# A graph layer and an expert layer on one core: the placing product moved to the end of TensorE's step, its addition behind VectorE's weighing

## The chip, the cores and the metric

The kernel runs on one NeuronCore of a Trainium2 chip. The metric is the device time of one execution in microseconds (us). Before the change it is 1864.92 us, the median of 7 runs (1861.53 to 1869.43).

## What is computed

The input is a matrix `x` of 6250 nodes with 256 values each and a list of 100,000 edges (`src`, `dst`), sorted by `dst`. Two layers are computed. The first is a graph attention layer with 8 heads: every node gathers the rows of the nodes that point to it, weighed by a softmax over its incoming edges, and a feed-forward net follows. The second sends every node through the two best of eight expert networks. In the reference, cut to what matters here:

```python
xn = layer_norm(x, ln1_g, ln1_b)
h = (xn @ W).reshape(N, HEADS, HEAD_DIM)
e = jax.nn.leaky_relu(a_src[src] + a_dst[dst], NEG_SLOPE)
ee = jnp.exp(e - emax[dst])
alpha = ee / denom[dst]
msg = h[src] * alpha[:, :, None]
agg = jax.ops.segment_sum(msg, dst, num_segments=N)      # the change is in how this sum is made
out = agg.reshape(N, HEADS * HEAD_DIM) + xn @ W_res + bias
out = layer_norm(out, ln2_g, ln2_b)
out = out + gelu_tanh(out @ ffn_w1 + ffn_b1) @ ffn_w2 + ffn_b2
# then, for every node: router, top 2 of 8 experts, weighted sum of their outputs
```

## The kernel before

**Preparation.** Up to about 150 us the kernel normalizes `x`, multiplies it by `W`, and writes a table of rows (`tab_s`: 256 values and 16 factors of the attention) to device memory. It also cuts the 782 tiles of 128 edges into 196 edge steps of four tiles. Since the edges are sorted by their target, the targets of some consecutive tiles lie close together. One to eight consecutive steps form a group, of which there are 110. The four tiles of a step write to four windows of 32 target rows each, and a whole group writes to at most 128 consecutive target rows, which straddle at most two of the 128-row blocks of the accumulators `acc_lo` and `acc_hi`. Groups are worked off from the last to the first: 66 groups with one step each, 31 with two, 9 with four and 4 with eight.

**The hand-written loop.** The loop at L1573 runs over a step number `s`. In each pass it issues one stage of several edge steps (a software pipeline, the list `STAGES` at L922), and after them, by `run_tasks` (L953), as many tasks of the node units and expert blocks as a budget per engine allows (`room`, from `ROOM` at L68; edge work is taken off it by `EDGES` and `BEHIND`). The stages of an entry `(f, d)` work on edge step `s - d`. Every engine executes its instructions in the order in which they are issued here; each engine has its own queue, and waits for another engine only where data or a buffer demand it. The stages are:

- `fetch` (L818, GpSimd): four indirect transfers that gather the source rows of an edge step into `gs` (four buffers).
- `spread` (L829, VectorE): the one-hot matrix `oh` of an edge step's targets within their windows; with the first step of a group also `qd`.
- `turn_spread` (L844, TensorE, then ScalarE): turns `oh` round in `pt` (one buffer, which the transpositions of the units, L982, share) and copies it.
- `give` (L851, TensorE): the product `pz`, which brings the targets' factors to the edges.
- `weigh` (L858, VectorE): three instructions, which multiply the gathered rows by their weights (`msg`).
- `add_tiles` (L872, TensorE): four products into `pl` (one buffer), summed over the steps of a group; behind the last step of a group ScalarE copies `pl` to `part` (two buffers).
- `place` (L896, VectorE, last step of a group only): the one-hot matrix `oh2` (two buffers) that says where the group's 128 sums belong within a block.
- `add_nodes` (L903, TensorE, last step of a group only): the placing product `p2` from `oh2` and `part`, at L906. `p2` has one buffer.
- `sum_up` (L910, VectorE, last step of a group only): reads the block's number into a register (L913), and adds `p2` to two neighbouring blocks by two instructions at L917.

**The order around the change.** Within a pass TensorE gets: `add_tiles`, `turn_spread`, `give`, `add_nodes`, then the tasks. VectorE gets: `sum_up` (of the product that TensorE got one pass earlier), `weigh`, `place`, `spread`, then the tasks.

**The tasks.** A first unit (L1187) multiplies two tiles of nodes by `W_res` into `py` (L1167, TensorE), and VectorE empties `py` with a bias added (`rg`, L1173). A node unit (L1207) divides the sums (L1054), normalizes them, and runs the feed-forward net: transpositions into `pt` (L982), a copy to `turned_in` by ScalarE (L989), products `ph` (L997), the gelu by ScalarE (`ht`, L1000), products `py` (L1007), which VectorE takes up (L1087). Then it normalizes again, routes (L1131 to L1145), and for every two units counts, ranks and lists tokens (up to `enlist`, L1323), a long run of small VectorE instructions. An expert block runs the same net with weights loaded for it, and VectorE empties `py` into `yb` (L1504). `py` has one buffer for all of them: a product into it can be issued in the same pass in which VectorE empties it, and waits for that.

Of the kernel before, what the change touches and what calls it, by code (L numbers as in the profile page):

```python
# [222 lines left out]
def gnn_moe_kernel(  # L223
# [66 lines left out]
    NG = len(order)  # L290
# [508 lines left out]
    def fetch_nodes(c):  # L799

        gq = bw.tile([P, W32 * 2 * H], F32, name="gq", bufs=1)
        nc.gpsimd.indirect_dma_start(
            out=gq, out_offset=None, in_=tab_q,
            in_offset=bass.IndirectOffsetOnAxis(ap=qrow[:, c:c + 1], axis=0))
        nc.sync.dma_start(tab_g[c * P:(c + 1) * P, :], gq)
        n = min(GC, NQ - c * GC)
        gd = bw.tile([P, GC, 2 * H], F32, name="gd")
        nc.sync.dma_start(gd[:, :n], tab_g[c * P:c * P + n * G, :].rearrange(
            "(g j) (r c) -> (j r) g c", j=G, r=W32))
        gds[c] = gd  # L810
# [91 lines left out]
    @behind_group  # L902
    def add_nodes(q):  # L903
        part, oh2 = live.pop((q, "part")), live.pop((q, "oh2"))
        p2 = bps.tile([P, DA], F32, name="p2")
        nc.tensor.matmul(p2, oh2, part, start=True, stop=True)  # L906
        live[q, "p2"] = p2

    @behind_group
    def sum_up(q):  # L910
# [4 lines left out]
        for b in range(2):  # L915
# [3 lines left out]

    STAGES = ((sum_up, 6), (weigh, 3), (add_tiles, 4), (place, 4), (turn_spread, 1), (give, 2),  # L922
              (spread, 0), (add_nodes, 5), (fetch, 0))
    LASTST = 6


# [26 lines left out]
    def run_tasks(s, room):  # L953

        more = True
        while more:
            more = False
            for t in list(pending):
                if (t.take in held or room[t.eng] <= 0.0
                        or any(d.step is None or d.step + gap > s for d, gap in t.deps)):  # L960
                    continue
                pending.remove(t)
                t.step = s
                room[t.eng] -= t.cost
                if t.take:
                    held.add(t.take)
                if t.free:
                    held.remove(t.free)
                t.fn()
                more = True  # L970
# [216 lines left out]
    def first_unit(u):  # L1187
        t0, n, _ = units[u]
        env = {}
        first_loads.append(task(lambda: load_first(t0, n, env), "SP", 0.0,  # L1190
                                [(d, 0) for d in back(firsts, 2)]))
        pr = task(lambda: first_product(n, env), "PE", 0.95 * n, [(first_loads[-1], 2)], take="py")
        ab = task(lambda: add_biases(n, env), "DVE", 0.7 * n,
                  [pr, *[(d, 0) for d in back(firsts, 1)]], free="py")
        firsts.append(task(lambda: store_first(t0, n, env), "SP", 0.0, [ab]))
# [3 lines left out]
    def node_loads(u):  # L1199
        t0, n, _ = units[u]  # L1200
        env = {"n": n}
        loads.append(task(lambda: load_nodes(t0, n, env), "SP", 0.0,
                          [(firsts[u], 0), *[(d, 0) for d in back(turned, 2) + back(added, 2)
                                             + back(normed, 3) + back(stores, 3)]]))
        return env
# [314 lines left out]
    def block_loads(i):  # L1520
        b = turn_of[i]
        env = {"n": 1 if NF <= b < NS else 2}
        env["units"], needs = next((u, d) for n, u, d in sure if n > b)
        free = [(d, 0) for d in blocks[i - 3:i - 2] + notes[i - 3:i - 2]] if i >= 3 else []

        env["pool"] = 1 if len(moew) > 1 and 1 not in pools[-2:] else 0
        user = [j for j in range(i) if pools[j] == env["pool"]][-2 + env["pool"]:][:1]
        if env["pool"] == 0 and pools.count(0) < 2:
            user = []
        pools.append(env["pool"])  # L1530
        env["lw"] = task(lambda: load_weights(b, env), "SP", 0.0,
                         [needs[-1], *[blocks[j] for j in user]])
        env["lx"] = task(lambda: load_block(b, env), "SP", 0.0, [*needs, *free])
        env["lp"] = task(lambda: load_params(b, env), "DVE", 0.4, [needs[-1], *free])
        ahead.append((b, env))
# [32 lines left out]
    s, u, since, was_nodes, loaded = 0, 0, [], False, {}  # L1568

    with tc.manual_schedule():  # L1570
        nc.sync.dma_start(xs[E * CAP:, :].rearrange("(p r) d -> p r d", r=2),
                          blank[:, None, :].to_broadcast([P, 2, DX]))
        while s < NG + LASTST or pending or u < len(units) or len(blocks) < NS:  # L1573
            for g in range(s, min(s + EARLY, NG)):
                if order[g][0] // GC not in gds:
                    fetch_nodes(order[g][0] // GC)
            for f, d in STAGES:
                if 0 <= s - d < NG:
                    f(s - d)
            if s == NG + LASTST:  # L1580
                edges.close()
                moew.append(gnn.enter_context(tc.tile_pool(name="moew3", bufs=1)))
            if len(firsts) < len(units) and len(firsts) <= s + 1:
                first_unit(len(firsts))
            if len(firsts) == len(units) and firsts[-1].step is not None and fp:
                first_.close()
                fp = None
            if last_hi and last_hi[0].step is not None and not moew and not fp:
                hi_pool.close()
                moew.append(ctx.enter_context(tc.tile_pool(name="moew", bufs=2, side="right")))  # L1590
            nb = len(blocks) + len(ahead)
            if moew and len(ahead) < 1 + len(moew) and nb < NS and any(n > turn_of[nb]
                                                                       for n, _, _ in sure):
                block_loads(nb)

            while sum(t.cost for t in pending if t.eng == "PE") < QUEUE:
                if (u < len(units) and units[u][2] <= s - LASTST
                        and not (ahead and was_nodes)):
                    was_nodes = True

                    if u == len(units) - 1:
                        urgent.append(0)
                    if u not in loaded:
                        loaded[u] = node_loads(u)
                    node_unit(u, loaded[u])
                    since.append(u)
                    u += 1
                    if u < min(len(units), len(firsts)):
                        loaded[u] = node_loads(u)
                    if u % 2 == 0 or u == len(units):  # L1610
                        chunk_tasks(since, u == len(units), u == len(units) - 1)
                        since = []
                    urgent.clear()
                elif ahead:
                    was_nodes = False
                    block_unit(*ahead.pop(0))
                else:
                    break
            room = dict(ROOM if s < NG + LASTST else ROOM_AFTER)
            if s < NG + LASTST:  # L1620
                g = s - 5
                ends = 0 <= g < NG and order[g][1] == groups[order[g][0]][1] - 1
                for e in EDGES:
                    room[e] -= EDGES[e] + ends * BEHIND[e]
            run_tasks(s, room)
            s += 1
            if there is None and final_list and final_list[0].step is not None and len(blocks) > NS - 2:
                there = nc.values_load(total[0:1, 0:1], min_val=0, max_val=NX)
        if NS < NX:
            with tc.If(there > NS):  # L1630
                while pending or len(blocks) < NX:
                    nb = len(blocks) + len(ahead)
                    if len(ahead) < 2 and nb < NX:
                        block_loads(nb)
                    if ahead:
                        block_unit(*ahead.pop(0))
                    run_tasks(s, dict(ROOM_AFTER))
                    s += 1
# [31 lines left out]
```

## Time and profile before

| | |
|---|---|
| median of 7 runs | 1864.92 us |
| profiled execution, its time | 1865.22 us |
| its span, first to last instruction | 1863.3 us |
| TensorE products busy | 1597.3 us, 86% |
| VectorE busy | 1080.1 us, 58% |
| GpSimd busy | 1113.7 us, 60% |
| ScalarE busy | 702.1 us, 38% |
| granted TensorE clock, mean | 0.942 |
| placing product L906: busy, idle before it | 82.4 us, 64.0 us, of them 63.9 for the addition L917 |
| addition L917 (220 instructions): busy, idle before them | 108.3 us, 127.3 us |

In profile lines the engines are PE (TensorE), PEld (its weight loads), DVE (VectorE), ACT (ScalarE) and POOL (GpSimd). A line of the timeline gives start and duration in us, engine, code line, operation, output and inputs, shape and count; in brackets stands the idle time of the engine just before it and what ended it. A line of the waits gives who waited for whom, total us, how often, and the longest. A line of a stretch gives its bounds and length, the busy time and the number of instructions of each engine, the granted clock of TensorE, the share of the DMA engines and GB/s. A float32 product is recorded as two matmul instructions. "issue" is time in which an engine waited for nothing that the profile shows.

### The profile page before, as it was taken

Reading aid. Unit: us, or ns where it says so; the run is one execution under the profiler, and the core shown is the slowest. Engines: PE = TensorE matmul, PEld = TensorE weight load, DVE = VectorE, ACT = ScalarE, POOL = GpSimd, SP = SyncE. Lnnn points to the kernel's source line nnn. Section 1 sums busy time; section 2 is a strip of 40 time slices with the busy share of each in tenths; the row PEclk is TensorE's granted clock in tenths of the full one; section 3 lists DMA queues with packets and bytes.
Section 4 is the critical chain, followed back from the end, with each engine's and each line's share of the span. In section 5 each row is a group of like instructions: output and inputs, shape, how many; then the busy total and the mean of one; then the engine's idle time right before and its main releaser. Section 6 shows DMA issues by size and latency. Waiting matters only on the chain. (4 is left out here: it accounts for less than half of the span.)

```text
span 1863.3 us, 28221 instructions
## 1 busy us (share of the span) xinstructions
PE 1597.3 (86%) x8479; PEld 1228.8 (66%) x8479; DVE 1080.1 (58%) x3959; ACT 702.1 (38%) x1621; POOL 1113.7 (60%) x1162
## 2 busy tenths in 40 slices
PE   4844787878787899999999999999999999899996
PEld 3523565656555677777777777777677777778885
DVE  8835888888888876575757564635544544131000
ACT  3830233233232343443444343443434433343332
POOL 2017765766656677767677777777777773321112
PEclk8977898889897999999999999999999999999998
DMA  3968755565445575756667666766668768648661
GB/s 117 294 206 219 232 159 152 165 173 175 146 141 169 155 225 156 232 155 189 173 175 213 200 184 192 225 196 206 207 187 248 224 154 227 200 104 274 188 190 39
DMA packets 246622, 347.86 MB, mean 187 GB/s; under 512 B 46033, under 2 KB 202865, under 8 KB 246460
## 3 DMA queue, kind: packets, MB, share of 16 engines
q1 hardware_dynamic: 184268, 203.16, 34.0%
q0 software_dynamic: 58880, 139.32, 29.2%
q10 hardware_dynamic: 3312, 3.48, 0.6%
q8 instruction: 70, 1.15, 0.3%
q14 instruction: 92, 0.75, 0.1%
HBM read 282.50 MB, written 67.26 MB: 188 GB/s over the span
## 5 line engine op out<-in xcount | busy, mean ns | idle before, releaser
L824 POOL DMA_INDIRECT gs<-tab_s,srce x784 | 803.5, 1025 | 349.8 <-issue 203.0
L997 PE MATMUL ph<-turned_in,w1b 128*128 128x256 f32 (+1 forms) x1696 | 388.8, 381 | 23.0 <-ACT ht L1000 17.6
L1007 PE MATMUL py<-w2b,ht 128*128 128x256 f32 x1648 | 370.8, 383 | 0.0
L997 PEld LDWEIGHTS ph<-turned_in,w1b 128*128 128x128 f32 x1696 | 301.4, 192 | 89.6 <-ACT ht L1000 35.1
L1007 PEld LDWEIGHTS py<-w2b,ht 128*128 128x128 f32 x1648 | 313.3, 192 | 41.9 <-DMA xs<-blank 0.4
L1514 POOL DMA_INDIRECT out_dram<-yb,tos x103 | 173.2, 1682 | 230.2 <-ACT yb L1510 104.9
L1000 ACT ACTIVATE ht<-ph,pc 128x256 f32<-128x256 f32 (+1 forms) x424 | 196.2, 467 | 243.4 <-PE ph L997 241.3
L866 DVE TENSOR_TENSOR msg<-gs,msg 128x1024 f32<-128x1024 f32 x196 | 240.4, 1226 | 6.7
L997 PE MATMUL ph<-turned_in,w_sb 128*128 128x256 f32 (+1 forms) x800 | 188.1, 384 | 8.9 <-ACT ht L1000 8.2
L1007 PE MATMUL py<-w_sb,ht 128*128 128x256 f32 x784 | 190.3, 402 | 4.1 <-DVE rg L1173 4.1
L1504 DVE TENSOR_TENSOR yb<-py,b2b 128x512 f32<-128x512 f32 (+1 forms) x53 | 35.8, 675 | 263.3 <-PE py L1007 245.1
L1007 PEld LDWEIGHTS py<-w_sb,ht 128*128 128x128 f32 x784 | 157.2, 203 | 28.2 <-DVE rg L1173 5.2
L997 PEld LDWEIGHTS ph<-turned_in,w_sb 128*128 128x128 f32 x800 | 145.1, 193 | 40.9 <-ACT ht L1000 15.0
L848 ACT ACTIVATE oht<-pt 128x128 f32<-128x128 f32 x196 | 53.9, 275 | 305.2 <-PE pt L846 267.0
L906 PE MATMUL p<-part,oh 128*128 128x264 f32 x220 | 82.4, 459 | 64.0 <-DVE acc_hi L917 51.8
L881 PE MATMUL pl<-msg,oh 128*32 128x264 f32 x1568 | 130.6, 405 | 6.4 <-DVE msg L866 6.3
L1405 POOL DMA_INDIRECT xs<-xe,slot x98 | 104.2, 1064 | 47.3 <-DMA w1b<-in_L_ffn_W_dram 23.8
L1000 ACT ACTIVATE ht<-ph,prm 128x256 f32<-128x256 f32 (+1 forms) x200 | 92.2, 469 | 104.5 <-PE ph L997 103.9
L885 ACT ACTIVATE part<-pl 128x264 f32<-128x264 f32 x110 | 42.7, 388 | 213.3 <-PE pl L881 209.8
L862 DVE TENSOR_TENSOR ww<-gs,pz 128x64 f32<-128x64 f32 x196 | 42.1, 215 | 138.3 <-PE pz L854 81.6
L846 PEld LDWEIGHTS pt<-ident,oh 128*128 128x128 f32 x196 | 27.6, 141 | 137.1 <-issue 76.2
L917 DVE SCALAR_TENSOR_TENSOR acc_lo<-p,here,acc_lo 128x264 f32 x112 | 55.2, 493 | 94.0 <-PE p L906 72.2
(335 smaller groups left out, 1928.9 us busy)
## 6 DMA issues: line engine op xcount, KB each, us to landing
w1b<-in_L_ffn_W_dram SPq DMA_DIRECT2D x53, 1024.0 KB
w2b<-in_L_ffn_W_dram SPq DMA_DIRECT2D x53, 1024.0 KB
xb<-xs SPq DMA_DIRECT2D x50, 260.0 KB
gs<-tab_s,srce POOLq DMA_INDIRECT x784
b2b<-in_L_ffn_b_dram SPq DMA_DIRECT2D x53, 128.0 KB
tab_s<-hg SPq DMA_DIRECT2D x12, 544.0 KB
xg<-in_x_dram SPq DMA_DIRECT2D x12, 512.0 KB
xt_d<-xt SPq DMA_DIRECT2D x12, 512.0 KB
```

The costliest lines, as they stand in the source:

```text
L824: nc.gpsimd.indirect_dma_start(out=gs[:, j, :], out_offset=None, in_=tab_s, in_offset=bass.IndirectOffsetOnAxis(ap=srce[:, t:t + 1], axis=0))
L848: nc.scalar.activation(oht, po[:, 0, :P], AF.Copy)
L866: nc.vector.tensor_tensor(msg[:, :, :D].rearrange("p t (h d) -> p t h d", h=H), gs[:, :, :D].rearrange("p t (h d) -> p t h d", h=H), msg[: ...
L881: nc.tensor.matmul(pl[j * W32:(j + 1) * W32, :], oh[:, j, :], msg[:, j, :], start=i == 0, stop=last)
L885: nc.scalar.activation(part, pl, AF.Copy)
L906: nc.tensor.matmul(p2, oh2, part, start=True, stop=True)
L917: nc.vector.scalar_tensor_tensor(to, p2, here[:, b, q:q + 1], to, op0=ALU.mult, op1=ALU.add)
L997: nc.tensor.matmul(ph[:, :W], w1[:, k, c * P:(c + 1) * P], env["in"][:, k, :W], start=k == 0, stop=k == KD - 1)
L1000: nc.scalar.activation(ht[:, :W], ph[:, :W], func, bias=b[:, c:c + 1], scale=1.0)
L1007: nc.tensor.matmul(env["py"][:, j, :], env["ht", c][:, j * P:(j + 1) * P], w2[:, c, :], start=c == 0, stop=c == KF - 1)
L1405: st = nc.gpsimd.indirect_dma_start(out=xs, out_offset=bass.IndirectOffsetOnAxis(ap=slots[k][:n, t:t + 1], axis=0), in_=xes[u // 2][:n, pl ...
L1514: st = nc.gpsimd.indirect_dma_start(out=out, out_offset=bass.IndirectOffsetOnAxis(ap=tos[:, b, j:j + 1], axis=0), in_=env["yb"][:, j, :], ...
```

## The change

The order of the stages is written anew. `sum_up` goes from the head of the list to its end, behind `spread`; `add_nodes` leaves the list and is called after `run_tasks`, so that it is the last that a pass issues. The distances stay: `add_nodes` works on edge step `s - 5`, `sum_up` on `s - 6`, the pass after. The budgets are as they were.

```diff
-    STAGES = ((sum_up, 6), (weigh, 3), (add_tiles, 4), (place, 4), (turn_spread, 1), (give, 2),
-              (spread, 0), (add_nodes, 5), (fetch, 0))
+    STAGES = ((weigh, 3), (add_tiles, 4), (place, 4), (turn_spread, 1), (give, 2), (spread, 0),
+              (sum_up, 6), (fetch, 0))
...
             run_tasks(s, room)
+
+            if 0 <= s - 5 < NG:
+                add_nodes(s - 5)
             s += 1
```

Within a pass TensorE now gets: `add_tiles`, `turn_spread`, `give`, the tasks, `add_nodes`. VectorE gets: `weigh`, `place`, `spread`, `sum_up`, the tasks.

## The prediction

> **What bounds the kernel now.** I first read the busy time by stretch. A step in what follows is one pass of the hand-written loop, numbered as in the code: the first addition (L917) falls in step 6. Up to step 71 every group has one edge step, so every step has a placing product (L906) and its addition; from step 72 on only every second, fourth or eighth step has.
>
> ```profile
> core 0: us, PE busy (x) PEld busy (x) DVE busy (x) ACT busy (x) POOL busy (x), PEclk, DMA share, GB/s
> 266.00:656.00 390.00, 313.42 (x1639) 233.25 (x1637) 326.29 (x1200) 123.62 (x290) 247.60 (x276) 0.88 0.54 158
> 656.00:1580.00 924.00, 868.26 (x4858) 669.49 (x4852) 520.71 (x1788) 374.63 (x829) 683.61 (x666) 0.99 0.68 198
> ```
>
> From 266 to 656 us (steps 22 to 71) VectorE (DVE) is busy 84%, TensorE (PE) 80%; from 656 to 1580 us TensorE is busy 94% and VectorE 56%. So in the first stretch VectorE's idle time is what lengthens the kernel, in the second TensorE's. The waits of the first stretch:
>
> ```profile
> PE p L906 <- DVE acc_hi L917: 41.5, 11, 5.5
> DVE acc_hi L917 <- PE p L906: 13.3, 8, 3.7
> PE py L1167 <- DVE rg L1173: 10.1, 6, 2.0
> DVE acc_hi L917 <- issue: 9.3, 14, 0.9
> ```
>
> TensorE waits at the placing product, since p2 has one buffer and VectorE has not yet added the previous one; VectorE waits for the placing product less often; and before the addition it also waits for "issue". That last wait is the load of the row number into a register (L913): its load takes 305 ns, its register work 190 and more. The trace shows it starting once the last instruction of the previous step's tasks has been handed over, so the addition begins 0.84 us after that instruction does (362.36 to 363.20 below).
>
> Then the timeline of both engines, which carries the estimate.
>
> ```profile
> 360.01 0.33 PE L854 MATMUL pz<-qd,oht 128*128 128x64 f32 x2
> 364.27 1.25 PE L906 MATMUL p<-part,oh 128*128 128x264 f32 x2 [3.93 <-DVE acc_hi L917]
> 367.02 3.78 PE L1167 MATMUL py<-wres,xtf 128*128 128x256 f32 x8 [1.50 <-DVE rg L1173]
> 371.31 0.65 PE L881 MATMUL pl<-msg,oh 128*32 128x264 f32 x8
> 373.72 5.43 PE L1007 MATMUL py<-w_sb,ht 128*128 128x256 f32 x24
> 379.08 0.66 PE L881 MATMUL pl<-msg,oh 128*32 128x264 f32 x8
> ```
>
> ```profile
> 362.36 0.16 DVE L1067 SCALAR_TENSOR_TENSOR nm<-mvc,rc 128x2 f32<-128x2 f32 x1
> 363.20 1.02 DVE L917 SCALAR_TENSOR_TENSOR acc_hi<-p,here,acc_hi 128x264 f32 x2 [0.67 <-issue]
> 364.14 0.21 DVE L862 TENSOR_TENSOR ww<-gs,pz 128x64 f32<-128x64 f32 x1
> 365.75 0.28 DVE L899 TENSOR_SCALAR oh<-jrow,snloc 128x128 f32<-128x128 f32 x1
> 366.28 0.68 DVE L1173 TENSOR_TENSOR rg<-py,bias_bc 128x512 f32<-128x512 f32 x1
> 367.48 1.02 DVE L917 SCALAR_TENSOR_TENSOR acc_hi<-p,here,acc_hi 128x264 f32 x2
> 370.84 0.69 DVE L1173 TENSOR_TENSOR rg<-py,bias_bc 128x512 f32<-128x512 f32 x1
> 375.06 1.02 DVE L917 SCALAR_TENSOR_TENSOR acc_hi<-p,here,acc_hi 128x264 f32 x2 [0.61 <-issue]
> ```
>
> These are steps 34, 35 and 36. See that rg (L1173) empties py, and TensorE's next py product, the bulk of its step, starts 0.06 us later; and that VectorE meanwhile goes on to the next step's addition without a wait (367.48).
>
> **The change, part by part.** No instruction is added or taken away, and the built order is the same on ScalarE, GpSimd and SyncE (so no DMA moves). On TensorE the placing product goes behind the step's tasks; on VectorE register load and addition go behind place and spread. One wait is new: in step s place (L899) writes an oh2 buffer, of which there are two, last read by the product of step s-1. Before, that product came early in TensorE's step and the addition had waited for it; now it is TensorE's last, so VectorE stops at L899, and behind it queue spread, the addition and all tasks of the step, on which TensorE's next tasks wait.
>
> *Removed.* In ten steps, 32 to 42 (additions at 344.94 and 424.12, 79.18 us), VectorE's waits sum to 7.95 us: register loads before six additions (0.96, 0.67, 0.61, 0.61, 0.67, 0.67), the product before two (0.56, 2.3), ACT res once (0.9). The load is now hidden behind weigh's 1.2 us instruction, unless L899 waits.
>
> *Added: step by step through the same ten.* Row intervals: addition to next instruction 0.94 (363.20 to 364.14); weigh to L899 1.61 (364.14 to 365.75); L899 and spread 0.54. So the addition is at weigh + 2.15; where L899 had to wait, I take 0.85 after the release (the 0.84 above), not 0.54. On TensorE 0.92 from add_tiles to the tasks, 0.70 from the product's start to its result (344.24 to 344.94). VectorE's tasks in steps 32 to 41 take 4.92, 5.46, 1.20, 2.61, 2.27, 4.91, 7.97, 6.67, 1.20, 2.72 us, from the timeline. Start as before: step 31 of TensorE at 343.32, tasks 2.26, product at 346.50, result 347.20; addition 32 at 348.05. Step 33's is at 348.05 + 0.94 + 4.92 + 2.15 = 356.06, step 34's at 364.61, its rg ends 366.23, weigh 35 starts 366.75. TensorE, held by that rg, runs its 4.29 us (367.02 to 371.31, so 366.29 to 370.58) and then the product: result 371.28. VectorE stood at L899 from 368.36: wait 2.92. Addition 35 at 372.13, rg ends 373.75; TensorE's 5.36 us end 379.16, result 379.86; VectorE from 377.29: wait 2.57. Addition 36 at 380.71, 37 at 386.07, 38 at 394.07, 39 at 405.13, 40 at 414.89 without waits (TensorE, no longer stopped by the product, is ahead). In step 40 rg ends 416.51; TensorE's 6.95 us (415.55 to 422.50 before) end 423.5, result 424.2; VectorE from 418.64: wait 5.56. Addition 41 at 425.05, 42 at 428.71 + 2.15 = 430.86. Ten steps: 430.86 - 348.05 = 82.8 against 79.2, +3.6. Waits of 11.1 us replace 7.95.
>
> The pattern (two steps with rg then a py product per unit of five steps) goes on through steps 22 to 71: 5 x 3.6 = **+18 us**. Steps 6 to 21, with few py products, I take at nothing; bounds -3 (loads saved) to +5 (one wait like step 40's).
>
> Bounds of the +3.6: TensorE's step 40 ran slow after idling (12 products in 6.95 us; in step 35 they took 5.36). At 5.36 the sum is +2.0. If step 35's run slowly too, +5.2. If the load after a wait is wholly hidden (0.54), 0.9 less. So +1 to +5.5, times five: +5 to +28.
>
> The Trainium skill (TensorE: Matmul & The Clock Gate, Part 1: The HAM clock gate) says that after an idle window of about 3.4 us the array runs at half clock until as long a busy one. Here 3.93 us of idle, a 1.25 us product and 1.50 us idle were followed by eight py instructions in 3.78 us, where others took 1.89, so the trace agrees. It speaks against the change: with the product gone from between them, the two gaps become one of some 6 us. By the rule alone steps 34, 39 and 40 stay slow, as I have them; by the full clock the sum would be 8 us smaller.
>
> *The second stretch.* TensorE's end of a step lies up to 6 us behind the point where VectorE would add, in 38 of 50 group steps. VectorE has 403 us idle there. Readers of py come 4.4 us or more before TensorE's next py product, but for a few at 1.6 to 2.6, all in steps without an addition, and the addition moves them by about 1 us (yb at 947.40 would start at 948.45). I cost this at nothing; without that cover 1 us a step. One gain: where a turn is TensorE's last task, add_tiles' successor L846 waits 0.53 us for turned_in (348.18 is such a row in the first stretch). The product now fills that gap; 15 group steps end so: 15 x 0.45 = **-7 us**. Bounds -7 to +8. From 1580 us nothing is moved.
>
> Sum, against the profiled execution (span 1863.3, time 1865.2): +18 - 7 = +11, **1876 us**; the median shown, 1864.92, is the same within 0.3.
>
> **Rivals.** *VectorE runs free.* If TensorE, no longer stopped 15 times for 53.6 us at the product, is so far ahead that its ends come in time, VectorE loses its waits: in the first stretch 15.7 (product), 13.0 (issue) and 5.9 us (same load, put down to PE ph), 34.6 in all. Half of it with the -7 gives 1841, all 1824. For it: those stops. Against: after the stop TensorE waits for rg anyway (1.50 at 367.02), and rg now stands behind the addition. It decides if VectorE waits under 0.8 us a step.
>
> *The second stretch pays too.* VectorE, held to TensorE's end in 38 steps, delivers late, and TensorE stops for py or a turn in half of them at 1.05 us, the length of the addition ahead of the tasks: +20, so 1865 + 18 - 7 + 20 = 1896. For it: enlist steps with 8 us of VectorE tasks. Against: the 4 to 18 us ahead of most py products. It decides once TensorE's idle there rises above today's 56 us.
>
> *A draw.* Lower bound of the ten steps (+1), times five, and -7: 1863. For it: saved loads against new waits. Against: the chain of step 40, which needs no fine number.
>
> That the edit does nothing is excluded by the built order.
>
> **How the numbers follow.** Forecast 0.57, VectorE free 0.20, draw 0.12, second stretch 0.11. What a measurement can tell from no change is 0.2%, 3.7 us. The forecast's own range is 1863 (+5 - 7) to 1891 (+28 + 5 - 7). The range, 1857 to 1896, leaves out four fifths of the free case and a third of the last, 0.2 in all. Faster: 0.20 and a little of the draw, 0.22; same 0.11; slower 0.67.
>
> **What would show it.** Additions of the first stretch without "issue" waits; VectorE idle before L899 some 5 to 6 us per unit; waits of L906 for L917 gone, those of py for rg grown; ten additions there some 83 us apart. In the second stretch idle before L846 shorter, TensorE's busy share unchanged. Wrong if the first stretch is not longer than 390 us, or if TensorE idles more after 656 us.

## The result, and the profile after

The changed kernel takes 1883.92 us (median of 18 runs, 1878.51 to 1891.33) against 1864.55 us (46 runs of the kernel before): ratio 1.0103 [1.0091, 1.0114]. The profiled execution took 1882.6 us, its span is 1880.7 us, 17.4 more than before; the mean granted clock is 0.940 against 0.942. In three later jobs (experiments 5 to 8) every kernel, the one before too (2133.7, 2096.7 and 2133.3 us), took 12 to 14% longer, at a granted clock of about 0.90 and with pauses of TensorE (one of 22.6 us in experiment 5) for which the traces show no cause, so from these only ratios within a job are told.

First the same two stretches by stretch of time, with the bounds moved along with the work (steps 22 to 71, and from there to the last edge steps):

```profile
core 0: us, PE busy (x) PEld busy (x) DVE busy (x) ACT busy (x) POOL busy (x), PEclk, DMA share, GB/s
276.00:681.00 405.00, 311.78 (x1618) 229.57 (x1617) 328.95 (x1200) 123.77 (x289) 240.34 (x272) 0.86 0.51 150
681.00:1600.00 919.00, 864.56 (x4876) 663.81 (x4875) 521.15 (x1793) 376.37 (x832) 693.82 (x668) 1.00 0.70 199
```

The first stretch grew from 390 to 405 us. VectorE issues the same 1200 instructions in it, but idles 76.1 us (405.00 - 328.95) instead of 63.7; TensorE idles 93.2 instead of 76.6. The second stretch shrank from 924 to 919 us, and TensorE idles 54.4 us in it where it had idled 55.7. So all of the loss comes before step 72.

The start of a step's weighing (L862), step by step in both timelines, tells more exactly where it comes from. The table also has the first four experiments, told below; each number is us later (+) or earlier (-) than in the kernel before, by the profiled executions:

| step | before, at us | changed | product alone | addition alone | three buffers | load ahead |
|---|---|---|---|---|---|---|
| 6 | 159.75 | -1.2 | -2.1 | -1.1 | +1.3 | +0.5 |
| 12 | 201.59 | -0.2 | +2.3 | -4.2 | -0.4 | -2.2 |
| 22 | 267.21 | +9.9 | +19.1 | -3.0 | +5.8 | -3.5 |
| 42 | 425.06 | +20.4 | +45.1 | -5.9 | +9.6 | -8.7 |
| 71 | 657.05 | +24.3 | +67.5 | -18.2 | +4.8 | -22.6 |
| 72 | 660.38 | +25.2 | +67.5 | -15.5 | +5.7 | -21.6 |
| 102 | 886.54 | +24.8 | +64.9 | -13.5 | +3.9 | -21.6 |
| 198 | 1561.52 | +19.5 | +60.7 | -16.6 | +1.4 | -17.4 |

The changed kernel loses some 10 us between steps 12 and 22, 14.4 between 22 and 71, and wins 5.7 back from step 72 on.

The waits from 150 to 690 us (waiter, released by; us in all, times, longest), first of the kernel before:

```profile
PE p L906 <- DVE acc_hi L917: 51.8, 18, 5.5
...
PE p L906 <- DVE acc_lo L917: 12.1, 4, 6.0
PE py L1167 <- DVE rg L1173: 11.9, 7, 2.0
DVE acc_hi L917 <- issue: 10.5, 16, 0.9
...
PE py L1007 <- DVE rg L1173: 4.1, 5, 1.2
...
DVE acc_lo L917 <- issue: 3.7, 5, 1.0
```

Then of the changed kernel; the bounds hold all its stops at place:

```profile
DVE oh L899 <- PE p L906: 65.9, 18, 7.2
...
PE py L1167 <- issue: 57.8, 10, 9.7
PE py L1007 <- DVE rg L1173: 23.8, 10, 8.3
...
PE p L906 <- DVE acc_hi L917: 13.4, 9, 6.0
...
DVE acc_hi L917 <- issue: 4.2, 15, 0.6
```

Its first line is new: VectorE stands at place until TensorE has run the product of the step before. The next two are TensorE's answer, 81.6 us of waiting for py to be emptied; before, its waits for rg in these bounds were 16.0 us (11.9 and 4.1). The first of these two is recorded as "issue", but the timeline below shows what ended it. The last two show what the change was paid with: TensorE's 63.9 us at the product have become 18.2 (13.4 here and 4.8 for `acc_lo`), the "issue" waits before additions 4.7 (4.2 and 0.5 for `acc_lo`) instead of 14.2 (10.5 and 3.7 before).

Both engines in steps 34 to 36, the steps that the prediction worked out:

```profile
369.60 1.95 PE L1167 MATMUL py<-wres,xtf 128*128 128x256 f32 x8
...
374.44 0.33 PE L854 MATMUL pz<-qd,oht 128*128 128x64 f32 x2
382.68 3.75 PE L1167 MATMUL py<-wres,xtf 128*128 128x256 f32 x8 [7.90 <-issue]
386.22 1.06 PE L982 MATMUL pt<-ident,xe 128*128 128x128 f32 x4
387.07 1.09 PE L906 MATMUL p<-part,oh 128*128 128x264 f32 x2
...
390.71 5.45 PE L1007 MATMUL py<-w_sb,ht 128*128 128x256 f32 x24 [0.44 <-DVE rg L1173]
396.00 0.61 PE L906 MATMUL p<-part,oh 128*128 128x264 f32 x2
```

```profile
381.89 0.68 DVE L1173 TENSOR_TENSOR rg<-py,bias_bc 128x512 f32<-128x512 f32 x1
...
383.09 0.21 DVE L862 TENSOR_TENSOR ww<-gs,pz 128x64 f32<-128x64 f32 x1
...
388.20 0.29 DVE L899 TENSOR_SCALAR oh<-jrow,snloc 128x128 f32<-128x128 f32 x1 [3.41 <-PE p L906]
...
389.04 1.02 DVE L917 SCALAR_TENSOR_TENSOR acc_hi<-p,here,acc_hi 128x264 f32 x2 [0.22 <-issue]
389.98 0.68 DVE L1173 TENSOR_TENSOR rg<-py,bias_bc 128x512 f32<-128x512 f32 x1
...
392.50 0.21 DVE L862 TENSOR_TENSOR ww<-gs,pz 128x64 f32<-128x64 f32 x1
...
396.64 0.29 DVE L899 TENSOR_SCALAR oh<-jrow,snloc 128x128 f32<-128x128 f32 x1 [2.44 <-PE p L906]
```

Read them crosswise. rg ends at 382.57 (381.89 + 0.68), and TensorE's py product starts 0.11 us later: the "issue" wait of 7.90 us is a wait for rg. VectorE weighs the next step and would be at place at 384.8, but TensorE's step has only begun; its last instruction, the product, ends at 388.16, and place starts 0.04 us later. Only then come spread, the register load, the addition, and behind them the rg of this step (389.98), for which TensorE is by then waiting again. Each engine waits for the other within one step, and neither can run ahead.

The eight py instructions after the 7.90 us took 3.75 us, where eight such took 1.95 in the step before (at 369.60); before the change, after 3.93 us of idle, a product and 1.50 us more, they had taken 3.78. The granted clock was 0.50 from 382.60 to 388.20 us, and in the kernel before 0.50 from 364.20 to 371.00. The Trainium skill (TensorE: Matmul & The Clock Gate, Part 1: The HAM clock gate) puts the array at half clock after an idle window of about 3.4 us; these rows agree, and the one long gap cost these eight instructions no more than the two shorter ones had.

### The profile page after: what moved, and what is told of

Same layout as the page of the kernel before. It is cut to its first block, busy times and chain, and to the rows that moved or that the text cites. A ratio compares the mean times of both kernels' runs of the same rounds, so it can differ in the third digit from the quotient of the medians.

```text
span 1880.7 us, 28146 instructions
## 1 busy us (share of the span) xinstructions
PE 1596.1 (85%) x8479; PEld 1221.0 (65%) x8479; DVE 1080.8 (57%) x3959; ACT 702.9 (37%) x1621; POOL 1118.3 (59%) x1162
## 5 line engine op out<-in xcount | busy, mean ns | idle before, releaser
L1007 PEld LDWEIGHTS py<-w2b,ht 128*128 128x128 f32 x1648 | 309.2, 190 | 40.4 <-issue 0.4
L1007 PE MATMUL py<-w_sb,ht 128*128 128x256 f32 x784 | 194.9, 409 | 23.8 <-DVE rg L1173 23.8
L997 PE MATMUL ph<-turned_in,w_sb 128*128 128x256 f32 (+1 forms) x800 | 189.2, 384 | 17.1 <-ACT ht L1000 14.1
L862 DVE TENSOR_TENSOR ww<-gs,pz 128x64 f32<-128x64 f32 x196 | 43.1, 220 | 153.5 <-PE pz L854 94.7
L1167 PE MATMUL py<-wres,xtf 128*128 128x256 f32 x196 | 68.1, 507 | 73.2 <-issue 57.8
L846 PEld LDWEIGHTS pt<-ident,oh 128*128 128x128 f32 x196 | 27.5, 140 | 125.7 <-issue 87.6
```

Of the source, the lines that this page charges most:

```text
L862: nc.vector.tensor_tensor(ww, gs[:, :, D:], live.pop((s, "pz")).rearrange("p (j c) -> p j c", j=G), op=ALU.mult)
L997: nc.tensor.matmul(ph[:, :W], w1[:, k, c * P:(c + 1) * P], env["in"][:, k, :W], start=k == 0, stop=k == KD - 1)
L1007: nc.tensor.matmul(env["py"][:, j, :], env["ht", c][:, j * P:(j + 1) * P], w2[:, c, :], start=c == 0, stop=c == KF - 1)
L1167: nc.tensor.matmul(py[:, j, :], env["xt"][:, j, k, :], wres[:, k, :], start=k == 0, stop=k == KD - 1)
```

## The experiments

Experiments 1 to 4 ran in one job on one chip, beside 17 runs of the kernel before (median 1864.92 us).

**1. The product alone.** The changed kernel, but the addition stays at the head of VectorE's step.

```diff
-    STAGES = ((weigh, 3), (add_tiles, 4), (place, 4), (turn_spread, 1), (give, 2), (spread, 0),
-              (sum_up, 6), (fetch, 0))
+    STAGES = ((sum_up, 6), (weigh, 3), (add_tiles, 4), (place, 4), (turn_spread, 1), (give, 2),
+              (spread, 0), (fetch, 0))
```

> The product goes to the end of TensorE's step as in the change; the addition stays at the head of VectorE's step. Theory (VectorE's stop for TensorE's end is the cost): the stop moves to the head of the step, so weigh, place and spread (2.15 us) wait behind it too. Some 18 stops of the first stretch get up to 2.15 us longer and more steps have one: 1905 to 1930 us. Rival (the addition ahead of the tasks delays rg by 0.94 us and with it TensorE's py products): the addition is ahead of weigh again, as before, so rg is no later than before: 1860 to 1870 us.

1927.06 us, ratio 1.0351 [1.0327, 1.0375]. Its waits in the same bounds:

```profile
DVE acc_hi L917 <- PE p L906: 87.8, 16, 8.9
...
DVE acc_hi L917 <- issue: 9.8, 15, 0.9
```

VectorE now stops at the addition, before it has weighed, and everything of its step stands behind that. With the 6.8 us for `acc_lo` these are 94.6 us in 19 stops, and the register loads are exposed again, as before the change. So TensorE's move by itself costs 62 us, and the addition's move doesn't cause the loss; in the changed kernel it takes back 43 us of it.

**2. The addition alone.** The kernel before, with the addition behind spread and the product in its old place.

```diff
-    STAGES = ((sum_up, 6), (weigh, 3), (add_tiles, 4), (place, 4), (turn_spread, 1), (give, 2),
-              (spread, 0), (add_nodes, 5), (fetch, 0))
+    STAGES = ((weigh, 3), (add_tiles, 4), (place, 4), (turn_spread, 1), (give, 2),
+              (spread, 0), (sum_up, 6), (add_nodes, 5), (fetch, 0))
```

> The addition goes behind spread as in the change; the product stays where it was before. Theory: no stop for TensorE's end, and the register load is hidden behind weigh. The first stretch loses its issue waits (13.0 + 5.9 us) and gains little else, TensorE's wait at the product grows but hides behind its wait for rg: 1845 to 1860 us. Rival (rg behind the addition): the 1 us by which rg comes later still holds up some 20 py products: 1875 to 1885 us.

1847.79 us, 0.9922 [0.9902, 0.9941]: 17 us faster than before. The waits, same bounds:

```profile
PE p L906 <- DVE acc_hi L917: 67.7, 18, 6.0
...
DVE ww L862 <- PE pz L854: 25.8, 13, 4.4
...
PE p L906 <- DVE acc_lo L917: 10.4, 4, 5.3
```

TensorE waits longer at its product than it did before (78.1 us; before 63.9), and the kernel is faster all the same: VectorE no longer waits before an addition, neither for the product nor for the load; its longest wait in these bounds is the 25.8 us for pz (4.9 before). The longer wait of TensorE, which isn't the limit of this stretch, cost nothing here. The change is thus two edits of opposite sign: the addition's, -17 us, and on top of it the product's, +36 (1883.9 - 1847.8).

**3. A third buffer for `oh2`.** The changed kernel, with which place need not wait for the product of the step before; one `oh` buffer less makes room.

```diff
-        oh = bw.tile([P, G, W32], F32, name="oh", bufs=6)
+        oh = bw.tile([P, G, W32], F32, name="oh", bufs=5)
...
-        oh2 = bw.tile([P, P], F32, name="oh2")
+        oh2 = bw.tile([P, P], F32, name="oh2", bufs=3)
```

> The change with three buffers for oh2 (and five for oh, not six, to make room). Theory: the addition still needs the product's result, so VectorE still stops, but at L917, with place, spread and the register load done: 0.8 us less at each of 18 stops, 1867 to 1875 us. Rival (the buffer of oh2 alone is the cost): the stops vanish, 1850 to 1865 us. Second rival (the slow clock after TensorE's longer gaps is the cost): no change, 1882 to 1886 us.

1865.85 us, 1.0012 [1.0000, 1.0024]: 18 of the 19 us are gone. That is 1 us below the range of the theory and 1 above that of the rival by which the stops vanish, so the time alone doesn't tell them apart; the waits do. First the waits, then VectorE in the steps shown above:

```profile
DVE acc_hi L917 <- PE p L906: 51.7, 15, 6.5
PE py L1167 <- issue: 51.6, 8, 8.8
...
DVE acc_lo L917 <- PE p L906: 8.8, 4, 4.0
```

```profile
376.37 0.28 DVE L899 TENSOR_SCALAR oh<-jrow,snloc 128x128 f32<-128x128 f32 x1
376.56 0.28 DVE L833 TENSOR_TENSOR oh<-jrow,loct 128x128 f32<-128x128 f32 x1
...
379.86 1.02 DVE L917 SCALAR_TENSOR_TENSOR acc_hi<-p,here,acc_hi 128x264 f32 x2 [2.88 <-PE p L906]
380.80 0.68 DVE L1173 TENSOR_TENSOR rg<-py,bias_bc 128x512 f32<-128x512 f32 x1
```

The stops are not gone: 60.5 us in 19 of them, against 65.9 in 18; 54.1 us in 17 are left if only those up to step 71 are counted, as all 18 of the changed kernel are. They have moved from place to the addition. Place, spread and the load now run ahead of the stop, and rg starts 0.94 us after its end instead of 1.78 (388.20 to 389.98). TensorE's pauses are still up to 8.8 us long, so the slow products after them, the rival's cause, are no explanation of the 18 us.

With experiment 1 this makes a series in which the work between the stop and the tasks differs. It is worked out from the intervals of the timelines: from an addition to the next instruction 0.94 us, from weigh to the addition 2.15, and from place's start to rg 1.78.

| the stop stands at | between its end and the tasks | time |
|---|---|---|
| the addition, at the head (1) | addition, weigh, place, spread: 3.1 us | 1927 us |
| place (the change) | place, spread, load, addition: 1.8 us | 1884 us |
| the addition, behind spread (3) | addition: 0.9 us | 1866 us |

From row to row 1.3 us are worth 43 us, and 0.8 us are worth 18. The first pair differs in one thing more, the exposed loads. VectorE's idle time from the weighing of step 6 to that of step 71 shows how much they are, and what a kernel wins or loses there is nearly all idle time, since VectorE's busy time there is 407 to 411 us in all six (in brackets, how many waits; the rest of the idle time is other waits and the short gaps between instructions):

| kernel | step 6 to 71 | VectorE idle | waits for the product (addition, place) | other waits before additions (the load) |
|---|---|---|---|---|
| before | 497.3 us | 88.0 | 16.7 (10) | 22.1 (33) |
| changed | 522.8 us | 111.9 | 65.9 (18) | 4.7 (18) |
| 1, product alone | 566.8 us | 158.6 | 94.6 (19) | 22.7 (33) |
| 2, addition alone | 480.2 us | 72.4 | 0 | 0 |
| 3, three buffers | 500.7 us | 92.9 | 54.1 (17) | 0 |
| 4, load ahead (below) | 474.1 us | 67.1 | 17.1 (10) | 0.3 (1) |

So 18 of the 43 us are loads (22.7 against 4.7), and 25 remain for 1.3 us of work behind the stop: 19 per us. The second pair gives 18 us for 0.84, 21 per us. With 17 to 19 stops this is about once per stop: what stands behind the stop is paid each time. It shows as longer stops (94.6, 65.9 and 54.1 us), which fits: TensorE's next tasks, and with them the product that VectorE will wait for, start that much later.

**4. The load ahead.** The kernel before, with only the register load moved: it is issued behind spread of the step before, ahead of the tasks, instead of directly ahead of the addition.

```diff
-        k = nc.vector.value_load(kfi[0:1, q:q + 1], min_val=0, max_val=half.shape[1] - 2)
+        k = live.pop((q, "k"))
...
+    @behind_group
+    def load_row(q):
+        half = acc_hi if q >= GHI else acc_lo
+        live[q, "k"] = nc.vector.value_load(kfi[0:1, q:q + 1], min_val=0,
+                                            max_val=half.shape[1] - 2)
...
-              (spread, 0), (add_nodes, 5), (fetch, 0))
+              (spread, 0), (load_row, 5), (add_nodes, 5), (fetch, 0))
```

> The kernel before, with the register load alone moved ahead: it stands behind spread of the step before, so ahead of that step's tasks. Theory: the issue waits ahead of the additions (13.0 us, and 5.9 put down to PE ph) are this load, and VectorE bounds the first stretch: 1846 to 1854 us, additions in that stretch without issue waits. Rival: VectorE then only waits for the product instead, 1860 to 1866 us.

1841.11 us, 0.9880 [0.9859, 0.9901]: the fastest of these kernels, 24 us faster than before, 43 faster than the changed kernel, and 5 better than expected.

```profile
PE p L906 <- DVE acc_hi L917: 34.6, 17, 4.2
...
DVE acc_hi L917 <- PE p L906: 17.1, 10, 3.7
```

No wait for "issue" is left before an addition. From 150 to 690 us the kernel before had 14.2 us of these (21 times), and 7.9 more (12 times) that stand as waits for PE ph; together 22.1, and this kernel is 22.6 us ahead at step 71. The load is thus most of what the addition's move had gained, and it can be had without letting the addition go ahead of rg. What makes experiment 2 6.7 us slower than this one, the addition ahead of rg or the waits for pz, wasn't separated.

**5 to 8: which part is worth keeping.** These ran in the three later jobs, beside the kernel before, so their expectations in us can't be tested.

Experiment 5 is experiment 2 with the product last in groups of more than one step only; experiment 6 the changed kernel with the change applied to groups of one step only (run twice); experiment 7 is experiment 4 with the later groups as in the changed kernel (run twice). The line that decides is, in 5 and 7 (in 6 it asks for `== 1`):

```diff
+    def steps_of(s):
+        return groups[order[s][0]][1]
...
+            if 0 <= s - 5 < NG and steps_of(s - 5) > 1:
+                add_nodes(s - 5)
```

Experiment 8 (run three times) is the changed kernel with three `oh2` buffers, in which the addition is VectorE's last as well, behind the tasks; a node unit is taken up one step later, so that its sums are complete:

```diff
-              (sum_up, 6), (fetch, 0))
+              (fetch, 0))
...
-                if (u < len(units) and units[u][2] <= s - LASTST
+                if (u < len(units) and units[u][2] <= s - LASTST - 1
...
             run_tasks(s, room)
+            if 0 <= s - 6 < NG:
+                sum_up(s - 6)
```

> As the kernel with the addition alone behind spread (1847.8 us), but for groups of more than one step (from step 72 on) the product is TensorE's last. Theory: there TensorE is the bound, the stops of VectorE cost nothing and the product fills the wait of L846 for turned_in, 5 us less: 1840 to 1845 us. Rival (late deliveries of VectorE hold up TensorE there as well): 1850 us or more.

> The whole change for groups of one step alone (to step 71); later groups as before. Theory: step 71 comes 24 us later than before, as with the change, and the 5 us of the later part are not won back: 1886 to 1892 us. Rival (the later part costs too): less than the change's 1884 us.

> The kernel of e6 again, for the same reason. Theory: step 71 comes 24 us later than before, and the 5 us of the later part are not won back: 1886 to 1892 us. Rival (the later part costs too): less than the change's 1884 us.

> As the kernel with the register load alone moved ahead (1841.1 us) for groups of one step; for later groups the product last and the addition behind spread. Theory: the two gains add up, 1833 to 1838 us. Rival: the later gain belongs to a VectorE that is behind, 1841 us or more.

> The kernel of e7 again, since in its first job the kernel before took 2134 us in place of 1865 us. If the kernel before takes about 1865 us. Theory: the gain of the load (to 1841 us) and the 5 us of the later part add up, 1833 to 1838 us. Rival: 1841 us or more.

> The change, but the addition is VectorE's last in a step, behind the tasks (three buffers of oh2, five of oh; node units are taken up one step later). The product is as late as in the change, and the same step's distance lies between. Theory (the cost is how much VectorE has still to do in the step behind its stop): nothing is behind the addition, by the end of VectorE's step TensorE's previous step has mostly ended, the stops go: 1850 to 1872 us. Rival (a product at the end of TensorE's step is what costs): 1880 us or more.

> The kernel of e8 again, for the same reason. Theory (the cost is the work that VectorE still has behind its stop): 1850 to 1872 us. Rival (a product at the end of TensorE's step is what costs): 1880 us or more.

> The kernel of e8 a third time, since in its first two jobs the kernel before took 2134 and 2097 us. If the kernel before takes about 1865 us. Theory (the cost is the work that VectorE still has behind its stop): 1850 to 1872 us. Rival (a product at the end of TensorE's step is what costs): 1880 us or more.

| experiment | first job | second job | third job |
|---|---|---|---|
| 5 | 0.9870 [0.9828, 0.9913] | | |
| 6 | 1.0061 [1.0027, 1.0095] | 1.0123 [1.0072, 1.0175] | |
| 7 | 0.9941 [0.9905, 0.9976] | 0.9966 [0.9925, 1.0007] | |
| 8 | 0.9947 [0.9911, 0.9982] | 1.0025 [0.9995, 1.0055] | 0.9990 [0.9956, 1.0024] |

Experiment 6 is slower than before in both jobs: the loss is in the groups of one step, as the table of steps has it. Experiment 8 is about 1% faster than 6 beside it, in both jobs: with the product last, but nothing of VectorE's tasks behind the stop, no loss can be seen. That fits the series above, but the ratios of its three runs lie on both sides of 1, and it has the three buffers with which experiment 3 left no loss either, so it settles nothing beyond experiment 3. Whether the product at the end of the later steps is worth having beside the early load (5 and 7) stays open: 7 isn't better than experiment 4's 0.9880, but the two weren't run in one job.

## Why the prediction was right, and which term was off

The predicted 1876 us was 8 short of the measured median, on the right side and inside the range. Step by step:

- **The new wait** (L899 for the product of the step before, everything behind it late) is what happened: 65.9 us in 18 stops, and experiments 1 and 3 show that the work behind the stop sets its price. For steps 35, 36 and 41 the working had 2.92, 2.57 and 5.56 us; the trace has 3.41, 2.44 and 5.29. The 0.85 us from release to addition, read from place's start, was 0.84 at the first two, 1.19 at the third (440.75 to 441.94), where the load stood exposed for 0.58.
- **Ten steps**: 82.8 us predicted, 83.7 measured (additions at 363.87 and 447.57).
- **Steps 22 to 71**: +18 predicted by five such units, +14.4 measured. From 276 to 681 us there were 13 stops of 45.5 us, where the five units would have 15 of 55; not every unit meets the step in the same phase.
- **Steps 6 to 21 are the mis-sized term.** They were taken "at nothing; bounds -3 to +5", because of "few py products". They cost about 10 us, twice the upper bound. The few are enough: there are five stops of 20.3 us in all, where VectorE had waited 1.8 us for the product before. The node units' py products begin at step 16, and the two longest stops, of 7.25 and 5.46 us, are in steps 17 and 21. The first of these two, in the changed kernel's timelines of both engines:

```profile
230.63 8.83 PE L1007 MATMUL py<-w_sb,ht 128*128 128x256 f32 x32 [2.14 <-DVE rg L1173]
239.30 0.61 PE L906 MATMUL p<-part,oh 128*128 128x264 f32 x2
```

```profile
229.80 0.68 DVE L1173 TENSOR_TENSOR rg<-py,bias_bc 128x512 f32<-128x512 f32 x1
...
231.00 0.21 DVE L862 TENSOR_TENSOR ww<-gs,pz 128x64 f32<-128x64 f32 x1
...
239.94 0.29 DVE L899 TENSOR_SCALAR oh<-jrow,snloc 128x128 f32<-128x128 f32 x1 [7.25 <-PE p L906]
```

  The same chain as in steps 34 to 41: rg, a py product of 32 instructions (8.83 us; 7.17 in the kernel before, after a shorter wait), the product behind it, VectorE at place. The pattern should have been started at the first unit whose py product follows an rg, and not at the bound of the chosen stretch.
- **The second stretch**: -7 predicted, -5.7 measured. The waits of L846 for turned_in went from 15.3 us (29) to 8.4 (16). The other two kernels with the product last win back there too, 6.8 (experiment 1) and 4.3 us (3), while those without it don't (2 wins 1.1, 4 loses 4.2). The cost of nothing for late additions held (the working counts 50 group steps there; the trace of the kernel before has 44 products L906): VectorE's waits for the product there grew from 69.7 to 124.5 us, and TensorE idles no more.
- **TensorE's stops at the product** were to be gone; 18.2 of 63.9 us stay, where its tasks of a step are shorter than VectorE's (0.64 us before the product at 373.05).
- **The rivals.** VectorE doesn't run free: it idles 12.4 us more in the first stretch. The draw needed +5 there. The second stretch doesn't pay: TensorE's idle there fell by 1.3 us.
- **The sum by what was measured**: +9.9 up to step 22, +14.4 to step 71, +0.9 to step 72, -5.7 to step 198, and 2.1 us won behind it, is the span's +17.4. That the total is only some 8 us off is in part luck: 10 too little at the start stands against 3.6 too much in the first stretch.

What the sum did not separate is the size of its gain. "Waits of 11.1 us replace 7.95" holds a saving by the hidden load; experiment 4 shows that the load had cost 24 us in all. The change wins most of this (the waits before additions fall from 22.1 to 4.7 us), and spends more than that, since the same edit raises VectorE's waits for the product from 16.7 to 65.9 us, ahead of the tasks.

## What to carry to other kernels

A wait between two engines that work step by step costs what stands behind it in the waiting engine's queue and is needed by the engine waited for: put the wait last, or at least behind the work that the other engine needs next, before trying to shorten it. When a product moves to the end of one engine's step, look for every buffer that it reads, and not only for its result, since the buffer's next writer inherits the wait. A register load ahead of an instruction belongs to an earlier place in the queue, behind which other work still runs.

## What the hardware showed that was not expected

The register load has 0.3 us in its own row, but moving it out of the addition's way saved 24 us, 22.6 of them up to step 71: additions had been held for 22.1 us in 33 cases, 0.67 us on average. In the kernel before, the load for the addition of step 34 starts at 362.4 us, with the last instruction of the tasks (362.36), and the addition only at 363.20, 0.8 us later. In the changed kernel one starts at 379.3, with weigh's long instruction (379.29), while place and spread are still to come, and its addition follows at 380.96 without a wait.

A wait named "issue" in the list need not be one: those of L1167 (57.8 us) end 0.1 us after an rg each time, and belong to VectorE.
